# A two-layer Perceiver block on one core: the order of TensorE's work in the two cross attentions, and the contexts' layer norm on VectorE

## The chip, the core and the metric

The kernel runs on one core of one Trainium2 chip. Its time is the device time of one execution in microseconds (us). Before the change the median of three runs is 2801.76 us (2800.55 to 2803.31). The five engines are called PE (TensorE, matrix products and transposes), DVE (VectorE), ACT (ScalarE), POOL (GpSimd) and SP (SyncE, which here only starts DMAs).

## The reference

64 batches of 32 tokens of width 256 pass through six steps, each added to its input: a cross attention to 256 context rows (plus one row of its own kind, and the 32 tokens themselves), a self attention, a mixture of 64 experts, a second cross attention, a second self attention and a small feed-forward step. All of it is in 32-bit floats. What the change touches is this:

```
xn = layernorm(ctx, ln_x_g, ln_x_b)            # (x - mean) / sqrt(var + eps) * g + b, 256 wide
k, v from xn and from the layer-normed tokens   # 16 heads of 64
kn = k / max(norm(k) / 8, eps) * kn_g           # a norm for each key and head
attn = softmax(qn @ kn.T);  out = attn @ v
...
x = x + tanh(((x_normed @ weight) @ aux1) @ aux2 + bias)   # the last step; the three matrices are multiplied first
```

## The kernel before, in words

The 2048 tokens are 16 **tiles** of 128 (4 batches of 32 each). A batch with its context is a **sequence** `s`, 64 in all; `t, b = divmod(s, 4)`.

The order of PE's instructions is that of the program text (`manual_schedule` on PE). The order on the other engines and on SP's queue is made by a planner at compile time from a cost model: it puts an instruction earlier when its data and buffers are free in the plan. `nc.any` copies go to ACT or DVE as the planner finds them idle. Each engine then runs its own list strictly in order. All PSUM results share eight banks (`bank`), so a matmul also waits until the bank it gets has been emptied.

**First cross attention** (`before`, L381 to L510; `CrossFirst`). For each sequence: `load` (one 256 KB DMA), `prepare` (layer norm with scale and bias, in place, on DVE then POOL), `turn` (4 transposes, then copies to `xT`), `keys` (32 products into 8 banks, copied to `kT` by DVE and ACT alternately; ACT squares each half into `sq`; four small DMAs fill `c3`), `norms` (16 products over the squares, then `nk` on DVE and ACT), `spread` (8 products, ACT exponentials), `scores` (32 products, then softmax on DVE and ACT), `weigh` (12 transposes of the softmax, copied to `at`), `values` (8 products of 512 columns and 4 for the tail rows, copied to `yT`). The steps are staggered: iteration `s` weighs sequence `s` while it builds keys and scores of `s + 2`, turns `s + 3` and prepares `s + 4`.

Between these steps stand **slots**. A slot runs one step of each open generator: first the tails, then the fronts. A *tail* is what follows for a finished tile (output projection, self attention, routing); a *front* is the query side of the next tile. A tile has 11 slots in this loop. They are called A1 (between keys and norms), A2 (after spread) and A3 (at the end; not for `b = 3`). The steps of a tail of tile `t` that matter here, counted in slots from A1 of the next tile's `b = 0`: 1 output heads, 2 output product, 3 layer norm, 4 its transposes, 5 query, key and value products, 7 transposes of these (A1 of `b = 2`), 8 self-attention scores (L573, A2 of `b = 2`), 9 softmax scaling and 32x32 transpose (`eT`), 10 products with the values (L310, A1 of `b = 3`), 11 the projection, 12 to 14 routing.

For tile 14 of 16 a tail waits `HOLD` slots after its step 2, so that it runs nearer to tile 15's tail, which has no loop left beside it.

**Experts** (`experts`). 64 experts, with a shared expert's steps between. At `e == AHEAD` (12) `after_weights` loads and multiplies out the weights of what comes later: first the latent attention's (`latent_weights`), then the feed-forward matrices (`ffn_weights`, L1047), whose three DMA loads take the space the former just gave back.

**Second cross attention** (`after`, L806; `CrossSecond`). The same idea with fewer steps. An iteration runs: load, `scores(s + 2)` (16 products, four banks, each reduced by DVE and then exponentiated by ACT), slot S1, `weigh(s)` (12 transposes, `at` copied by ACT or DVE), slot S2, `values(s)` (8 products), slot S3. Its generators are `queries` (the query side, two tiles ahead) and `follow` (output projection, self attention and feed-forward of a finished tile, the latter's HOLD as above).

Of the kernel before, what the change touches and what calls it, by code (L numbers as in the profile page):

```python
# [10 lines left out]
F32 = mybir.dt.float32  # L11
# [3 lines left out]
ALU = mybir.AluOpType  # L15
AX = mybir.AxisListType

P = 128
D = 256
S = 32  # L20
# [3 lines left out]
H = 16  # L24
# [3 lines left out]
LAT = 32  # L28
# [1 line left out]
CAP = 128  # L30
GT = 4
AHEAD = 12
HOLD = 5
TOPK = 8
FI = 128
FS = 512
# [50 lines left out]
def done(steps):  # L87
    for _ in steps:
        pass


class Kernel:
# [116 lines left out]
            k0 += n  # L209
        return [at[:n, j, :] for j, n in enumerate(sizes)]  # L210

    def weighed(self, yT, b, at, values, tail=None):

        nc = self.nc
        ps = [self.bank("psY") for _ in range(2)]
        n = len(at)
        for kc in range(2):
            for i in range(n):  # L220
                nc.tensor.matmul(  # L221
                    ps[kc],
                    lhsT=values[i][:, kc * P : (kc + 1) * P],
                    rhs=at[i],
                    start=(i == 0),
                    stop=(i == n - 1 and tail is None),
                )
        if tail is not None:
            for kc in range(2):
                r = slice(64 * kc, 64 * kc + 64)  # L230
                nc.tensor.matmul(ps[kc], lhsT=tail[1][r, :], rhs=tail[0][r, :], start=False, stop=True)  # L231
        for kc in range(2):
            nc.any.tensor_copy(  # L233
                yT[:, kc, :, b * S : (b + 1) * S], ps[kc].rearrange("p (h i) -> p h i", h=H)
            )

    def heads_out(self, t, yT, wv, wo, bias, split=False):

# [52 lines left out]
    def attend_self(self, t, e, recip, wo, bias):  # L291

        nc = self.nc
        v = self.vz[t % 2]
        nc.vector.tensor_tensor(e, e, recip.unsqueeze(2).to_broadcast([P, H, S]), ALU.mult)  # L295
        eT = self.wk.tile([P, H, S], F32, name="eT", bufs=self.eb)
        nc.vector.transpose(eT.rearrange("p a b -> p (a b)"), e.rearrange("p a b -> p (a b)"))
        yield
        if self.slack:
            yield  # L300


        ps = [self.bank("psY") for _ in range(NB)]
        for k in range(2):
            for odd in range(2):
                for g in range(4):
                    h = 8 * k + 2 * g + odd
                    for b in range(NB):
                        r = slice(b * S, (b + 1) * S)
                        nc.tensor.matmul(  # L310
                            ps[b][g * 32 : (g + 1) * 32, k * S : (k + 1) * S],
                            lhsT=v[r, h, :, :].rearrange("p a b -> p (a b)"),
                            rhs=eT[r, h, :],
                            start=(odd == 0),
                            stop=(odd == 1),
                        )
        oT = self.wk.tile([P, 2, P], F32, name="oTs", bufs=self.vb)
        for b in range(NB):
            nc.any.tensor_copy(
                oT[:, :, b * S : (b + 1) * S], ps[b][:, : 2 * S].rearrange("p (k i) -> p k i", k=2)  # L320
            )
        yield
        ps = self.bank("psY")
        self.product(ps[:, :D], [oT[:, k, :] for k in range(2)], [wo[:, k, :] for k in range(2)])
        self.add_to_x(t, ps[:, :D], bias)
# [46 lines left out]
    def before(self, ctx):  # L372
# [3 lines left out]
        tc, nc, a = self.tc, self.nc, self.a  # L376
# [3 lines left out]
        w = self.pool(ctx, "w0", 1)  # L380
# [29 lines left out]
        ps = self.bank("psT")  # L410
# [9 lines left out]
        next(first)  # L420
        next(first)
        cross.prepare(1)
        for i in range(2):
            cross.load(i + 2)
            cross.turn(i)
            cross.keys(i)
            cross.norms(i)
            done(first)
            cross.spread(i)
            cross.scores(i)  # L430
        cross.load(4)
        cross.prepare(2)
        cross.prepare(3)
        cross.turn(2)

        wv = self.load(w, "wv", [P, 2, HD], a["a_wv"].rearrange("(k p) n -> p k n", p=P))
        wo = self.load(w, "wo", [P, 8, D], a["a_wo"].rearrange("(k p) n -> p k n", p=P))
# [38 lines left out]
        def slot():  # L476
            for q in (tails, fronts):
                for g in list(q):
                    if next(g, q) is q:
                        q.remove(g)  # L480

        for s in range(n):
            t, b = divmod(s, NB)
            next(zeros, None)
            if b == 0 and t + 3 < self.nt:
                self.tokens(t + 3)
            if b == 0 and t + 1 < self.nt:
                fronts.append(cross.queries(t + 1))
            if s + 5 < n:
                cross.load(s + 5)  # L490
            if s + 2 < n:
                cross.keys(s + 2)
            cross.weigh(s)
            slot()
            if s + 2 < n:
                cross.norms(s + 2)
            cross.values(s)
            if s + 2 < n:
                cross.spread(s + 2)
            slot()  # L500
            if s + 3 < n:
                cross.turn(s + 3)
            if s + 2 < n:
                cross.scores(s + 2)
            if s + 4 < n:
                cross.prepare(s + 4)
            if b == NB - 1:
                tails.append(self.tail(t, cross.yT, wv, wo, bo, sw, swo, sg, gw))
            else:
                slot()  # L510
# [5 lines left out]
    def tail(self, t, yT, wv, wo, bo, sw, swo, sg, gw):  # L516

        yield from self.heads_out(t, yT, wv, wo, bo, True)
        yield
        if t == self.nt - 2:  # L520

            for _ in range(HOLD):
                yield
        yield from self.self_first(t, sw, swo, sg)
        yield from self.route(t, gw)
# [130 lines left out]
    def experts(self, ctx, slot, tails):  # L656
# [94 lines left out]
        for e in range(E):  # L751
            weigh(e + AHEAD)
            fetch(e + 3)
            turn(e + 2)
            while (at - total + rest) * E < rest * e:
                next(side)
                at += 1
            inner(e + 1)
            outer(e)
            if e == AHEAD:  # L760
                self.after_weights()
        done(side)

        side, sums = shared(nt // GT - 1), self.combine(0)
# [32 lines left out]
    def after_weights(self):  # L797
        a, w = self.a, self.w2
        wq = self.load(w, "wq", [P, 2, HD], a["b_wq"].rearrange("(k p) n -> p k n", p=P))
        wkT = self.load(w, "wkT", [P, 8, D], a["b_wkT"].rearrange("(k p) n -> p k n", p=P))  # L800
        wv = self.load(w, "wv", [P, 2, HD], a["b_wv"].rearrange("(k p) n -> p k n", p=P))
        wo = self.load(w, "wo", [P, 8, D], a["b_wo"].rearrange("(k p) n -> p k n", p=P))
        bo = self.row(w, "bo", a["b_bo"], D)
        self.weights = wq, wkT, wv, wo, bo
        self.lat = self.latent_weights(w)
        self.ffnw = self.ffn_weights(w)  # L806

    def after(self, ctx):
        self.eb = self.vb = 1
# [15 lines left out]
        def slot():  # L825
            for g in list(steps):
                if next(g, steps) is steps:
                    steps.remove(g)
# [8 lines left out]
        for s in range(n):  # L837
            t, b = divmod(s, NB)
            if s + 3 < n:
                cross.load(s + 3)  # L840
            if s + 2 < n:
                cross.scores(s + 2)
            if b == NB - 2 and t + 2 < self.nt:
                steps.append(cross.queries(t + 2))
                if t + 3 < self.nt:
                    steps.append(self.combine(t + 3, 3))
            slot()
            cross.weigh(s)
            slot()
            if s < 2:  # L850

                slot()
                slot()
            cross.values(s)
            if b == NB - 1:
                steps.append(self.follow(t, cross.yT, wv, wo, bo))
            slot()
# [3 lines left out]
    def follow(self, t, yT, wv, wo, bo):  # L861

        yield from self.heads_out(t, yT, wv, wo, bo)
        if t == self.nt - 2:

            for _ in range(HOLD):
                yield
        yield from self.self_second(t, *self.lat)
        yield from self.ffn(t, *self.ffnw)
# [100 lines left out]
    def self_second(self, t, wl, bl, wvo, bvo, wqk, bqk, wo, bo):  # L970
        nc = self.nc
        _, zT = yield from self.normed(t)
        lat = self.wk.tile([P, 2 * H, LAT], F32, name="lat", bufs=1)
        latf = lat.rearrange("p h l -> p (h l)")
        for n in range(2):
            ps = self.bank("psA")
# [102 lines left out]
class CrossFirst:  # L1079
# [76 lines left out]
    def prepare(self, s):  # L1156

        k, nc, cx = self.k, self.k.nc, self.cx[s]
        k.layernorm(cx, cx)
        nc.gpsimd.tensor_tensor(cx, cx, self.gx.unsqueeze(1).to_broadcast([P, 2, D]), ALU.mult)  # L1160
        nc.gpsimd.tensor_tensor(cx, cx, self.bx.unsqueeze(1).to_broadcast([P, 2, D]), ALU.add)

    def turn(self, s):

# [110 lines left out]
        at = k.keyed(sim, [P, P, P])  # L1275
        self.weights = at[:2], [cx[:, 0, :], cx[:, 1, :]], (at[2], c3)

    def values(self, s):
        k = self.k
        b = s % NB  # L1280
        if b == 0:
            self.yT = k.wkx.tile([P, 2, H, P], F32, name="yT", bufs=1)
        k.weighed(self.yT, b, *self.weights)


class CrossSecond:
# [185 lines left out]
```

## Time and profile before

| what | value |
|---|---|
| profiled execution | 2804.67 us |
| its span (first to last instruction) | 2802.8 us, so 1.87 us lie around it |
| median of the runs | 2801.76 us |
| ACT, POOL busy | 1241.6 us (44%), 684.3 us (24%) |
| mean granted PE clock | 0.982 |
| first cross attention | about 0 to 1535 us |
| last tails, experts | about 1535 to 1800 us |
| second cross attention and the rest | about 1800 to 2803 us |
| PE busy, 160 to 1500 us | 1312.38 of 1340 us |
| PE busy, 1830 to 2700 us | 849.40 of 870 us |

A busy PE is not PE at its peak, since the ends of its matmuls are modelled: one matmul's modelled end lies past the start of the next. So where PE stalls, the idle time shown is a little less than the time lost, and the distance from one start to the next is the better measure. The granted clock says at what part of full speed PE was let run. Idle time of another engine costs nothing by itself; what it does to PE shows in the waits of PE.

### The profile page before, as it was taken

The numbers are of one execution on the slowest core, as the hardware profiler recorded it, in microseconds if no ns is written. First come the engines' busy times: TensorE is split into PE (matmuls) and PEld (weight loads), VectorE is DVE, ScalarE is ACT, GpSimd is POOL, SyncE is SP. The second block draws the span as 40 slices with busy tenths as digits, with TensorE's granted clock in tenths as the row PEclk, the third lists the DMA queues.
The fourth block names the chain that finished last, engine by engine and source line by source line (L and its number), as shares of the span: only waits on it lengthen the run. The fifth ranks groups of instructions, "written<-read, shape, count | busy, mean of one in ns | idle before, by whom it ended". The sixth has DMA issues, their size and how long they took to land. (4 is left out here: it accounts for less than half of the span.)

```text
span 2802.8 us, 58905 instructions
## 1 busy us (share of the span) xinstructions
PE 2657.6 (95%) x23386; PEld 1824.5 (65%) x23386; DVE 1694.9 (60%) x4427; ACT 1241.6 (44%) x3436; POOL 684.3 (24%) x756
## 2 busy tenths in 40 slices
PE   6999999999999999999999799999999999999996
PEld 3556666666666666666666578667777777777764
DVE  5546666666666666666665433466666666666664
ACT  3455555555555555555554223333333333333331
POOL 5211333133313331243121200321212222121001
PEclk8999999999999999999999899999999999999997
DMA  8000011011000000000001677321211222222110
GB/s 271 16 14 18 31 33 31 18 31 33 29 18 27 26 22 18 20 19 16 18 7 38 233 237 243 91 67 54 58 51 50 59 52 58 56 51 55 33 35 5
DMA packets 136087, 157.03 MB, mean 56 GB/s; under 512 B 24024, under 2 KB 118979, under 8 KB 135812
## 3 DMA queue, kind: packets, MB, share of 16 engines
q1 hardware_dynamic: 114308, 119.65, 13.8%
q0 software_dynamic: 12288, 25.21, 3.4%
q10 hardware_dynamic: 9216, 8.39, 0.9%
q8 instruction: 185, 3.03, 0.4%
q14 instruction: 90, 0.74, 0.1%
HBM read 121.63 MB, written 37.75 MB: 57 GB/s over the span
## 5 line engine op out<-in xcount | busy, mean ns | idle before, releaser
L167 PE MATMUL psA<-xT,wk 128*128 128x289 f32 x2048 | 517.4, 411 | 7.9 <-ACT xT L1176 4.5
L167 PEld LDWEIGHTS psA<-xT,wk 128*128 128x128 f32 x2048 | 388.0, 191 | 134.8 <-issue 21.8
L780 POOL DMA_INDIRECT y<-oute,idx x128 | 131.5, 1028 | 643.4 <-DVE x L791 453.9
L167 PE MATMUL psA<-at,cx 128*128 128x512 f32 x512 | 235.4, 602 | 20.0 <-ACT qTl L1005 18.2
L221 PE MATMUL psY<-at,cx 128*128 128x512 f32 x512 | 239.8, 612 | 0.1
L167 PE MATMUL psY<-xT,qk 128*128 128x257 f32 x1024 | 234.3, 382 | 0.0
L167 PEld LDWEIGHTS psY<-xT,qk 128*128 128x128 f32 x1024 | 190.8, 190 | 35.0 <-issue 10.2
L1357 DVE TENSOR_REDUCE mx<-psY 128x1 f32<-128x257 f32 x256 | 105.7, 423 | 133.6 <-PE psY L167 133.5
L1358 ACT ACTIVATE sim<-psY,mx 128x257 f32<-128x257 f32 x256 | 121.6, 476 | 142.3 <-DVE mx L1357 142.2
L184 ACT ACTIVATE sim<-sim,mx 128x289 f32<-128x289 f32 x256 | 134.1, 526 | 100.0 <-DVE mx L182 100.0
L221 PEld LDWEIGHTS psY<-at,cx 128*128 128x128 f32 x512 | 93.5, 192 | 123.0 <-issue 108.8
L167 PEld LDWEIGHTS psA<-at,cx 128*128 128x128 f32 x512 | 92.9, 190 | 120.8 <-issue 76.7
L233 ACT COPY yT<-psY 128x512 f32<-128x512 f32 x127 | 68.2, 589 | 220.7 <-PE psY L231 220.7
L645 POOL DMA_INDIRECT buf<-z,fi x128 | 126.5, 988 | 148.0 <-DVE fi L642 102.2
L1160 POOL TENSOR_TENSOR cx<-cx,a_gx 128x512 f32<-128x512 f32 x64 | 81.8, 1278 | 292.1 <-DVE cx L140 290.3
L1206 ACT ACTIVATE sq<-kT 128x1156 f32<-128x1156 f32 x128 | 149.4, 1167 | 4.4 <-DVE kT L1203 2.8
L1201 ACT COPY kT<-psA 128x289 f32<-128x289 f32 x256 | 94.8, 389 | 104.2 <-PE psA L167 104.2
L1376 ACT COPY at<-psT 128x512 f32<-128x512 f32 x145 | 78.8, 595 | 123.4 <-PE psT L1375 118.3
L1218 PE MATMUL psB<-sq,c 128*32 128x289 f32 x1024 | 109.4, 419 | 19.7 <-ACT sq L1206 19.5
L1388 DVE SCALAR_TENSOR_TENSOR yT<-at,xT,psA 128x512 f32<-128x512 f32 x128 | 94.0, 735 | 56.1 <-PE psA L167 50.7
L167 PE MATMUL psY<-yT,wv 128*64 128x128 f32 x2048 | 121.6, 275 | 1.6 <-DVE yT L1388 1.4
L1177 POOL COPY xT<-lnT 128x64 f32<-128x64 f32 x64 | 15.3, 240 | 423.0 <-PE psA L167 299.3
(257 smaller groups left out, 5190.5 us busy)
## 6 DMA issues: line engine op xcount, KB each, us to landing
cx<-in_ctx SPq DMA_DIRECT2D x128, 256.0 KB
we<-in_m_ew SPq DMA_DIRECT2D x64, 384.0 KB
xT<-in_ctxT SPq DMA_DIRECT2D x64, 257.0 KB
buf<-zero SPq DMA_DIRECT2D x32, 256.0 KB
be<-buf SPq DMA_DIRECT2D x64, 128.0 KB
oute<-oe ACTq DMA_DIRECT2D x64, 128.0 KB
mu<-in_mask SPq DMA_DIRECT2D x16, 128.5 KB
x<-in_x SPq DMA_DIRECT2D x16, 128.0 KB
```

Source lines behind the costliest of these rows:

```text
L167: self.nc.tensor.matmul(ps, lhsT=lhs[i], rhs=rhs[i], start=(i == 0), stop=(i == n - 1))
L184: nc.scalar.activation(sim[:, g, :], sim[:, g, :], AF.Exp, bias=mx[:, g : g + 1], accum_out=sm[:, g : g + 1])
L221: nc.tensor.matmul(ps[kc], lhsT=values[i][:, kc * P : (kc + 1) * P], rhs=at[i], start=(i == 0), stop=(i == n - 1 and tail is None),)
L645: d = nc.gpsimd.indirect_dma_start(out=self.buf[:, :], out_offset=bass.IndirectOffsetOnAxis(ap=fi[:, k : k + 1], axis=0), in_=z[:, 0, :], ...
L780: nc.gpsimd.indirect_dma_start(out=y, out_offset=None, in_=self.oute[:, :], in_offset=bass.IndirectOffsetOnAxis(ap=self.idx[:, t, k : k + ...
L1160: nc.gpsimd.tensor_tensor(cx, cx, self.gx.unsqueeze(1).to_broadcast([P, 2, D]), ALU.mult)
L1201: nc.scalar.copy(kT[:, p, :], ps[:, :JK])
L1206: nc.scalar.activation(sq[p // 4], kT[:, p - 3 : p + 1, :], AF.Square)
L1218: nc.tensor.matmul(ps[g * 32 : (g + 1) * 32, :JK], lhsT=k.pair[odd], rhs=sq[p // 4][:, p % 4, :], start=(odd == 0), stop=(odd == 1),)
L1357: nc.vector.tensor_reduce(mx[:, g : g + 1], ps[:, :J], AX.X, ALU.max, negate=True)
L1358: nc.scalar.activation(sim[:, g, :], ps[:, :J], AF.Exp, bias=mx[:, g : g + 1], accum_out=sm[:, g : g + 1])
L1388: nc.vector.scalar_tensor_tensor(self.yT[:, c, :, b * S : (b + 1) * S], self.at[:, 2, :].rearrange("p (h i) -> p h i", h=H), xT[:, c, J - ...
```

## The change

It has seven parts: the order of PE in the first cross attention's loop, with the values cut in two halves and the norms between them; the same work's start-up; the contexts' layer norm, whose scale and bias move from POOL into DVE's own operations; one more slot in the self attention of the first layer (`attend_self`); the two HOLD counts, with a second buffer for `lat`; the feed-forward weights, built at expert 24 instead of 12; and in the second cross attention, `weigh(s)` ahead of `scores(s + 2)`.

```diff
-HOLD = 5
+HOLD = 8, 9
...
-    def weighed(self, yT, b, at, values, tail=None):
+    def weighed(self, yT, b, kc, at, values, tail):
...
+        if kc == 0:
+            self.psy = [self.bank("psY") for _ in range(2)]
+        ps = self.psy
+        for i in range(len(at)):
+            nc.tensor.matmul(
+                ps[kc], lhsT=values[i][:, kc * P : (kc + 1) * P], rhs=at[i], start=(i == 0), stop=False
+            )
+        if kc == 1:
+            for c in range(2):
+                r = slice(64 * c, 64 * c + 64)
+                nc.tensor.matmul(ps[c], lhsT=tail[1][r, :], rhs=tail[0][r, :], start=False, stop=True)
...
@@ attend_self
         yield
-        if self.slack:
-            yield
+        yield
...
@@ before, start-up
-        for i in range(2):
-            cross.load(i + 2)
-            cross.turn(i)
-            cross.keys(i)
-            cross.norms(i)
-            done(first)
-            cross.spread(i)
-            cross.scores(i)
-        cross.load(4)
+        for i in range(2, 5):
+            cross.load(i)
+        cross.turn(0)
+        cross.keys(0)
+        done(first)
+        cross.turn(1)
+        cross.norms(0)
         cross.prepare(2)
+        cross.spread(0)
+        cross.scores(0)
+        cross.keys(1)
+        cross.turn(2)
+        cross.norms(1)
         cross.prepare(3)
-        cross.turn(2)
+        cross.spread(1)
+        cross.scores(1)
...
@@ before, the loop
+            cross.weigh(s)
             if s + 2 < n:
                 cross.keys(s + 2)
-            cross.weigh(s)
             slot()
+            cross.values(s, 0)
             if s + 2 < n:
                 cross.norms(s + 2)
-            cross.values(s)
+            cross.values(s, 1)
             if s + 2 < n:
                 cross.spread(s + 2)
...
@@ tail, follow
-            for _ in range(HOLD):
+            for _ in range(HOLD[0]):
...
-            for _ in range(HOLD):
+            for _ in range(HOLD[1]):
...
@@ experts, after_weights
+            if e == 2 * AHEAD:
+                self.ffnw = self.ffn_weights(self.w2)
...
-        self.ffnw = self.ffn_weights(w)
...
@@ after, the loop
-            if s + 2 < n:
-                cross.scores(s + 2)
...
             slot()
             cross.weigh(s)
+            if s + 2 < n:
+                cross.scores(s + 2)
             slot()
...
@@ self_second
-        lat = self.wk.tile([P, 2 * H, LAT], F32, name="lat", bufs=1)
+        lat = self.wk.tile([P, 2 * H, LAT], F32, name="lat")
...
@@ CrossFirst.prepare
-        k.layernorm(cx, cx)
-        nc.gpsimd.tensor_tensor(cx, cx, self.gx.unsqueeze(1).to_broadcast([P, 2, D]), ALU.mult)
-        nc.gpsimd.tensor_tensor(cx, cx, self.bx.unsqueeze(1).to_broadcast([P, 2, D]), ALU.add)
+        mv, rs = k.stats(cx, 2)
+        for j in range(2):
+            x = cx[:, j, :]
+            nc.vector.scalar_tensor_tensor(x, x, mv[:, j, 0:1], self.gx, ALU.subtract, ALU.mult)
+            nc.vector.scalar_tensor_tensor(x, x, rs[:, j : j + 1], self.bx, ALU.mult, ALU.add)
```

## The prediction

> **What bounds the kernel now.** I read the page's first two parts, then PE's waits, then the timeline around the longest of them.
>
> ```profile
> PE 2657.6 (95%) x23386; PEld 1824.5 (65%) x23386; DVE 1694.9 (60%) x4427; ACT 1241.6 (44%) x3436; POOL 684.3 (24%) x756
> PE   6999999999999999999999799999999999999996
> PEclk8999999999999999999999899999999999999997
> ```
>
> PE is the bound in every slice but the first, the last and the move to the experts. No edit removes a matmul, so a gain must come out of PE's idle time (2802.8 - 2657.6 = 145 us) or its half-clock time. The waits name the idle time (total, times, longest):
>
> ```profile
> PE psB L1218 <- ACT sq L1206: 19.5, 23, 2.1
> PE psA L167 <- ACT qTl L1005: 18.2, 12, 1.7
> PE psY L310 <- DVE at L208: 14.7, 14, 1.3
> PE psA L167 <- DMA f_a<-in_f_a: 4.8, 1, 4.8
> PE psB L573 <- ACT yT L233: 2.7, 14, 0.2
> ```
>
> Twelve to fourteen times means once a tile. The timeline (start, length, matmuls, idle before) shows the size, first cross attention first:
>
> ```profile
> 310.40 0.68 PE L1218 MATMUL psB<-sq,c 128*32 128x289 f32 x4
> 311.94 1.17 PE L1218 MATMUL psB<-sq,c 128*32 128x289 f32 x12 [0.86 <-ACT sq L1206]
> ...
> 330.72 0.26 PE L310 MATMUL psY<-eT,vz 32*32 32x32 f32 x6
> 332.01 1.24 PE L310 MATMUL psY<-eT,vz 32*32 32x32 f32 x122 [1.04 <-DVE at L208]
> 333.18 1.86 PE L1218 MATMUL psB<-sq,c 128*32 128x289 f32 x16
> ```
>
> The unbroken 16 take 1.86 us, the broken ones 2.71 (310.40 to 313.11): 0.85 lost. L310 takes 2.53 us here and 1.29 unbroken in the second layer: 1.24 lost. The second cross attention (weigh, values, then the next slot):
>
> ```profile
> 2252.83 1.48 PE L1375 MATMUL psT<-c,sim 128*128 128x128 f32 x12
> 2255.80 3.67 PE L167 MATMUL psA<-at,cx 128*128 128x512 f32 x8 [1.50 <-ACT qTl L1005]
> 2259.31 1.02 PE L167 MATMUL psB<-qTl,wqk 128*128 128x512 f32 x2
> 2260.17 0.60 PE L1014 MATMUL psT<-c,lat 128*128 128x128 f32 x4
> 2260.60 0.38 PE L149 MATMUL psT<-c,z 128*128 128x128 f32 x2
> 2260.82 3.64 PE L167 MATMUL psY<-xT,qk 128*128 128x257 f32 x16
> 2264.39 1.29 PE L1026 MATMUL psB<-kTl,qf 32*32 32x32 f32 x128
> ```
>
> Twelve transposes pace at 0.109, 1.31 in all; the values start 2.97 after them, so 1.66 is lost.
>
> **1. Loop order and the extra slot.** Before, keys, weigh, A1, norms; now weigh, keys, A1, first half of the values, norms. The norms' wait is for ACT's second square. At `b = 2` its cover after keys was weigh (1.31) and A1; now A1 and half the values (4 of 8 products at 0.43, 1.72). Scores also lie one weigh further from keys, so the softmax ahead of the square on ACT starts 1.31 earlier against keys. Together 1.7 us against 0.85: gone. What is late next is `b = 3`: A1 held L310, which moves to A2, so its cover is the half values alone. In the trace ACT ends that square at 333.82 (start 332.65, 1.17), with its exponentials back to back from 327.9. Keys would end near 330.9, the second norms start near 333.1: up to 0.7 comes back a tile. The split adds no change of PE's array shape: full to 32 columns and back happened once already. After the norms `nk` (DVE 0.46, ACT 0.45) has the second half (1.72) and the tail (1.13) as cover instead of 4.8; 2.9 suffices.
>
> L310's wait is for a bank that weigh's copies (L208) hold. In A2 it stands where L573 stands, behind spread with the values' copies just issued: that row costs 0.2. Its `eT` has a slot more. So 1.24 becomes about 0.25.
>
> Per tile: 1.0 + 0.85 - 0.35 (half of 0.7) = 1.5, times 14 = 21; I take **-20**, ends -28 and -5.
>
> **2. Layer norm on DVE.** Per context POOL loses 1278 + 1270 ns, which fed nothing late. DVE loses two tensor_scalars and gains four two-tensor operations; the nearest row is the experts' sum, same size, all in SBUF:
>
> ```profile
> L140 DVE TENSOR_SCALAR cx<-cx,mv,rs 128x256 f32<-128x256 f32 x128 | 61.8, 515 | 7.4 <-ACT rs L120 7.4
> L791 DVE SCALAR_TENSOR_TENSOR x<-y,w,x 128x256 f32<-128x256 f32 x128 | 59.8, 467 | 0.3
> ```
>
> 4 x 0.467 - 2 x 0.515 = 0.84 us, 54 us of DVE in all. The Trainium skill speaks against this: VectorE: DVE Perf Modes, The perf-mode tier table, has fp32 tensor_scalar in SBUF at two elements a cycle and the two-tensor operation at one. By it the removed pair would be worth about 2 x 0.23 and the addition 1.4 us, 90 in all. The row disagrees: median 411 ns with its pointer scalars, hardly under 467, and up to 1422 while POOL worked. I take the row. DVE is at 854 of 1340 us in this loop, so its cover is slack: **0**. Bounds: -13 (if the stretch of 515 over 411 is gone, 0.1 x 128, and had been on the path) and +54.
>
> **3. Start-up and first tile.** At 22.85 two tensor_scalars take 2.26 us beside POOL's multiply; the query sums on DVE, ACT's second query square and the copy to `xT` queue behind, and keys(0) starts at 26.97 after 3.40 idle, then partly at half clock (9.73 us for 32 products against 8.07). Without POOL I expect 2 of the 3.4 and 1.7 of clock back. keys(1) and keys(2) lose waits of 0.68 and 0.82 for `xT`, norms(0) its 1.08; spread(0) loses its cover (+1.1), norms(1) waits more for a softmax now closer. The loads of contexts 2 to 4 go ahead of keys' eight `c3` DMAs and the mask on SP, 768 KB at 271 GB/s, 2.8 us, wanted late. **-6**, ends -11 and +2.
>
> Until tile 0's tail exists no slot has filler: from 70 to 160 us PE idles 9.4, on squares (0.80, 1.98, 0.80, 2.10) and on `xT` before keys (0.75, 0.65, 1.80, 0.54), and the clock falls twice:
>
> ```profile
> 119.84:123.25 3.41, 1.53 (x16) 0.54 (x16) 1.56 (x3) 2.98 (x5) 1.39 (x2) 1.00 0.12 39
> 123.25:126.66 3.41, 3.41 (x8) 1.42 (x5) 0.46 (x1) 0.45 (x1) 0.36 (x3) 0.50 0.00 0
> ```
>
> (PE busy is the third number, clock third from the end.) The Trainium skill (TensorE: Matmul & The Clock Gate, Part 1) halves the clock after an idle window of about 3.4 us; by that, stalls of 2 us would cost only themselves, 9.4. Here a window with PE busy 1.53 of 3.41 was enough, and eight values take 5.16 instead of 3.70: 1.5 more, twice. Half the values now cover the squares and weigh covers `xT`: 12.4 at most; **-7**, ends -11 and -3.
>
> **4. Feed-forward weights.** The 4.80 idle, then half clock (16 products in 6.25 us against 3.6), sum 7.4. The three loads issue at 1628.5, when the latent weights free their space; SP's planner had brought the latent loads forward by some 60 us (1552), so at expert 24, over 30 us later, these have landed. A copy of `mid` (0.37) shows now, 0.5. **-7**; 0 if they stay at their place in the text behind the expert loads.
>
> **5. weigh before scores.** Scores (3.64) stand between weigh and values, and ACT's `at` copies no longer queue behind the exponentials: 12 x 1.66 + two short ones, -21. But S3 and S1 now touch. At `b = 2` to `3`, `kTl` (0.16 for the last transpose to end, 0.1 to signal, copy 0.59) has only L149's two transposes (0.22) before L1026: 0.6; at `b = 0` to `1`, `zT` waits likewise before the latent products. The nearest row, at the end of the kernel, has transposes at 2756.72 and products at 2757.62 0.90 from start to start less 0.22 of their own; less another tile's two transposes, 0.5. So 1.1 x 13 = 14 comes back: **-7**, ends -21 and +3.
>
> **6. HOLD and lat.** Tile 14's steps move nearer tile 15's, but ahead of them in each slot: its query or latent products (2.75 and 4.6 us) now delay tile 15's output product by what the loop saves. Beside the softmax (idle 6.15 and 7.53) more of tile 14 stands, on a DVE both share. The second `lat` only makes this overlap possible. **0** and **+1**, each -4 to +5.
>
> Sum: -20 + 0 - 6 - 7 - 7 - 7 + 0 + 1 = -46. The profiled 2804.67 becomes 2759; the median of the runs lies 2.9 lower: **2756**.
>
> **Rivals.** *Nothing comes back*: part 5 whole (-21): 2742. For: ACT is idle at S3; against: the copies have latency. *Half is given back*: part 1 brings 10 only, since `b = 3` pays its 0.7 and other norms wait too (+10); start-up brings 1 (+5), the two ends cost 6 more: 2777. For: softmax and squares share ACT; start-up is full of DMA (271 GB/s). *Slower*: DVE queues are planned, and the four operations (1.9 us) can stand before the key copies or `nk`. At 327.83 DVE copies keys PE began at 321.4, so there it is late. In half the 64 contexts that is 61 us: 2817; it decides from 24 contexts (46 / 1.9). Against: only `b = 2` and `3` are that tight. *The loads are not brought forward*, so that part 4 does nothing: 2763, inside the first case.
>
> **Chances.** About 2756 (2744 to 2769) 0.45; nothing back 0.13; half back 0.27; slower 0.12; within 0.2% (about what a measurement can tell) 0.03. Faster 0.85. The range 2730 to 2792 leaves out the slower cases.
>
> **What would show it.** Right: L310's wait under 4 us in all, no `f_a` wait, `qTl` gone from PE's waits, `kTl` and `zT` in its place near 14 us; L1218 under 10; DVE near 1750 busy, POOL near 520. Wrong: PE waiting for key copies or `nk`; a new wait on `at` or banks at weigh; a half clock at 55 us as before.

## The result, and the profile after

The changed kernel takes 2813.70 us (median of six, 2811.40 to 2815.39) against 2801.61 for the kernel before (six runs): 1.0041 times as long, 95% interval 1.0028 to 1.0053. It was forecast 46 us faster and is 12 slower. First its page: span, busy time and the PE rows of the 40 slices.

```profile
span 2812.1 us, 59021 instructions
...
PE 2655.0 (94%) x23386; PEld 1823.0 (65%) x23386; DVE 1664.0 (59%) x4432; ACT 1306.7 (46%) x3559; POOL 552.9 (20%) x628
...
PE   6999999999999999999997899899999999999995
...
PEclk9999999999999999999998899999999999999996
```

The matmuls are the same 23386. PE's idle time (span less busy) has grown from 145.2 to 157.1 us. Of the clock's dips at the start only the one near 55 us is left, half as long (the clock from 50 to 70 us was 0.66 and is 0.83); those at the move to the experts and at the end have stayed. PE's waits (total, times, longest):

```profile
PE psT L149 <- DVE z L140: 28.1, 9, 6.4
PE psB L1223 <- ACT sq L1211: 24.2, 33, 2.3
PE psB L1029 <- DVE qf L1014: 18.2, 13, 3.8
...
PE psY L306 <- issue: 4.3, 4, 1.8
PE psA L167 <- issue: 4.1, 3, 1.7
PE psB L575 <- issue: 3.9, 1, 3.9
...
PE psY L306 <- ACT yT L230: 3.4, 14, 0.2
...
PE psT L207 <- DVE qk L541: 3.2, 11, 0.5
```

L310 is now L306, and its 14.7 us on `at` are 3.4. `qTl` and `f_a` are gone. But the norms (L1218, now L1223) wait 24.2 instead of 19.5, `qf` takes exactly the 18.2 that `qTl` had, and "issue" appears: PE waits for nothing that the profile shows. Before, that was 3.4 us in all.

Where the time went, by the start of the same PE work in both traces (after less before, us):

| marker | difference | so this stretch |
|---|---|---|
| output heads of tile 0 (at 166 before) | -16.0 | start-up and tile 0: -16.0 |
| output heads of tile 14 (1475) | -12.7 | 14 tiles of the first loop: **+3.3** |
| output heads of tile 15 (1526) | -15.7 | here HOLD puts off steps of tile 14: -3.1 |
| first shared expert (1568) | -5.8 | last tails: **+9.9** |
| first scores of the second loop (1786) | -9.9 | experts: -4.0 |
| values of sequence 60 (2717) | -0.6 | second loop: **+9.2** |
| end of PE (2794) | +9.2 | last tails: **+9.9** |

So the start gave what was forecast (13) and 3 more, the experts a little over half of their 7; the first loop, put at -20, gave nothing, and three places lost. Its quiet tiles are 0.1 us shorter than before on average, but four others (tiles 2, 3, 8 and 13) 0.6 to 1.4 longer. Here is a tile of the first loop, from keys to scores at `b = 3` (timeline of PE after):

```profile
499.61 4.31 PE L167 MATMUL psA<-xT,wk 128*128 128x289 f32 x17
503.76 1.88 PE L222 MATMUL psY<-at,cx 128*128 128x512 f32 x4
505.57 0.68 PE L1223 MATMUL psB<-sq,c 128*32 128x289 f32 x4
507.04 1.17 PE L1223 MATMUL psB<-sq,c 128*32 128x289 f32 x12 [0.79 <-ACT sq L1211]
...
511.81 0.28 PE L306 MATMUL psY<-eT,vz 32*32 32x32 f32 x6
512.34 1.40 PE L306 MATMUL psY<-eT,vz 32*32 32x32 f32 x122 [0.25 <-ACT yT L230]
```

Between the last key product and the norms there is only the half of the values: A1 is empty. The norms take 2.64 us from 505.57 to their end. Unbroken they take 1.19, which the prediction had not seen: its "unbroken" 1.86 already held 0.67 of a wait that the modelled ends hide.

The losses of a quiet tile (from the output heads of tile 5 to those of tile 6; norms: start to end less 1.19; L306: start to the next instruction less 1.22), in us, are these. `old_dve` (the kernel before with the layer norm on DVE) and `order_again` (the changed kernel without the slot, with the old HOLD and the old second loop) are told of below:

| | before | `old_dve` | after | `order_again` |
|---|---|---|---|---|
| norms at b = 2 | 1.36 | 1.01 | 0.28 | 0 |
| norms at b = 3 | 0.67 | 0.67 | **1.45** | 0.03 |
| norms at b = 0 | 0 | 0 | 0 | 0 |
| norms at b = 1 | 0.65 | 0.66 | **1.10** | 0 |
| L310 / L306 | 1.24 | 1.24 | 0.65 | 0 |
| weigh, for a bank | 0 | 0 | 0.41 | 0 |
| sum | 3.92 | 3.58 | 3.89 | 0.03 |
| the whole tile | 93.54 | 93.19 | 93.40 | 89.97 |

Differences of the sums follow those of the tiles within 0.4 us. The changed kernel moved 3.9 us of stalls about and removed almost none.

### The profile page after: what moved, and what is told of

Same layout as the page of the kernel before. It is cut to its first block, busy times and chain, and to the rows that moved or that the text cites. A ratio compares the mean times of both kernels' runs of the same rounds, so it can differ in the third digit from the quotient of the medians.

```text
span 2812.1 us, 59021 instructions
## 1 busy us (share of the span) xinstructions
PE 2655.0 (94%) x23386; PEld 1823.0 (65%) x23386; DVE 1664.0 (59%) x4432; ACT 1306.7 (46%) x3559; POOL 552.9 (20%) x628
## 5 line engine op out<-in xcount | busy, mean ns | idle before, releaser
L167 PE MATMUL psA<-xT,wk 128*128 128x289 f32 x2048 | 510.8, 407 | 1.3 <-issue 1.1
L222 PE MATMUL psY<-at,cx 128*128 128x512 f32 x512 | 248.6, 609 | 0.0
L1223 PE MATMUL psB<-sq,c 128*32 128x289 f32 x1024 | 99.8, 415 | 24.2 <-ACT sq L1211 24.2
L167 PEld LDWEIGHTS psY<-yT,wv 128*64 128x64 f32 x2048 | 113.2, 137 | 9.7 <-issue 4.8
L167 PE MATMUL psY<-wo,oT 128*128 128x256 f32 x512 | 118.8, 386 | 0.3 <-issue 0.3
L1272 DVE TENSOR_TENSOR sim<-psB,sim 128x289 f32<-128x289 f32 x256 | 101.2, 448 | 29.2 <-PE psB L1263 29.1
```

The source lines that it names most:

```text
L167: self.nc.tensor.matmul(ps, lhsT=lhs[i], rhs=rhs[i], start=(i == 0), stop=(i == n - 1))
L222: nc.tensor.matmul(ps[kc], lhsT=values[i][:, kc * P : (kc + 1) * P], rhs=at[i], start=(i == 0), stop=False)
L1223: nc.tensor.matmul(ps[g * 32 : (g + 1) * 32, :JK], lhsT=k.pair[odd], rhs=sq[p // 4][:, p % 4, :], start=(odd == 0), stop=(odd == 1),)
L1272: nc.vector.tensor_tensor(sim[:, g, :], ps[i][:, :JK], sim[:, g, :], ALU.mult)
```

## The experiments

Each run is compared with the kernel before on the same chip; "ratio" is that comparison with its 95% interval, and a hundredth of it is 28 us.

**HOLD alone undone** (`hold5`).

```diff
-HOLD = 8, 9
+HOLD = 5, 5
```

> The changed kernel with both HOLD counts at 5 again, all else as changed. Theory H (the longer HOLDs put tile 14's steps in front of tile 15's): the move to the experts gives back 8 to 10 us and the end another 8 to 10, so 2795 (2790 to 2801). Rival (the two ends lose by PE's code fetch, wherever the dense bursts fall): some 'issue' waits move, the time stays within 5 us of 2814.

2797.3 us, ratio 0.9977 [0.9967, 0.9986]: 18 less than the changed kernel (1.0041). Its last stretch loses 0.3 us against the kernel before, where the changed kernel loses 9.9. Step 6, put at 0 and +1, costs 18.

**The second loop's order undone** (`second_old`).

```diff
+            if s + 2 < n:
+                cross.scores(s + 2)
             if b == NB - 2 and t + 2 < self.nt:
...
             cross.weigh(s)
-            if s + 2 < n:
-                cross.scores(s + 2)
```

> The changed kernel with scores(s + 2) ahead of the first slot again in the second cross attention, all else as changed. Theory as predicted blind (weigh first is worth 7): 2821, PE waits 1.5 us a tile for at behind qTl. Theory now (weigh first gains 0.2 us a tile and then loses 10 to code fetch and the half clock behind it): 2804 (2800 to 2810), with no wait on qf at L1029 and tiles of 61.5 us without outliers.

2805.5 us, ratio 1.0006 [0.9997, 1.0015]: the new order costs 10 where it was to gain 7. All tiles take 61.53 to 61.55 us. With the new order (timeline of PE after), where the third column is the engine and the bracket the idle time before:

```profile
2125.68 1.02 PE L167 MATMUL psB<-qTl,wqk 128*128 128x512 f32 x2
2126.53 0.60 PE L1017 MATMUL psT<-c,lat 128*128 128x128 f32 x4
2126.97 0.38 PE L149 MATMUL psT<-c,z 128*128 128x128 f32 x2
2128.56 1.28 PE L1029 MATMUL psB<-kTl,qf 32*32 32x32 f32 x128 [1.20 <-DVE qf L1014]
2129.76 0.82 PE L167 MATMUL psA<-zT,wq 128*128 128x128 f32 x5
2132.31 4.79 PE L167 MATMUL psA<-zT,wq 128*128 128x128 f32 x27 [1.73 <-issue]
```

S3 and S1 touch, as foreseen, and the latent scores (L1029) wait; but it is `qf` that comes last, which DVE makes from the product at 2125.68, and not `kTl` or `zT`. So a quiet tile takes 61.37 us, 0.17 less than before. The 1.73 <-issue behind them is the other loss: six of the tiles take 62.4 to 65.0. Each of the six has one such wait, 7.3 us in all, and behind two of them (at 2132 and 2279 us) the clock is 0.50 for 3.4 us.

**A slot between latent keys and latent scores** (`second_slack`), HOLD 5 and 5, to give that wait its cover.

```diff
         nc.any.tensor_copy(kT, ps)
         yield
+        yield
```

> The changed kernel with HOLD 5 and 5, and one more slot between the copies of the latent keys and the latent scores; the second loop keeps its new order (weigh ahead of scores). Theory (qf's wait, 1.20 us in 13 tiles, came back only because slots S3 and S1 now touch): the wait goes, quiet tiles fall from 61.4 to 60.2, 2797 - 15 = 2782, with some tiles still 1 to 3 us longer for PE's own instructions. Rival (another wait takes its place, z, zT or the copies' bank): quiet tiles stay at 61.4 and the time at 2797.

2797.4 us, ratio 0.9981 [0.9974, 0.9988]: the rival. `qf` is gone from PE's waits, but two others stand in its place, and all tiles but one take 61.97:

```profile
PE psA L167 <- ACT zT L150: 17.5, 31, 0.7
...
PE psY L167 <- DVE yT L1393: 7.4, 15, 0.9
```

It looks as if, with S3 and S1 together, some step of the tail always stands too near to its data; that is argued from these waits alone.

**32 tiny products in front** (`pad32`), all else equal, to see what "issue" is. The trace shows them as 64 products and 64 weight loads.

```diff
-        ps = self.bank("psT")
+        ps, i = self.bank("psT"), self.ident[:32, :32]; [nc.tensor.matmul(ps[:32, 256:288], lhsT=i, rhs=i, start=True, stop=True) for _ in range(32)]
```

> The changed kernel with 32 tiny products (128 PE instructions[...]) put in front of the first transpose, where PE idles for 16 us anyway; the order on every engine is otherwise the same. Theory F (the 'issue' waits of PE are waits for its code): the waits leave tiles 2, 3, 8 and 13 of the first loop and turn up in other tiles, and the sum over the kernel changes; total 2805 to 2822. Rival (they are waits for data that the profile does not name): the same tiles are long by the same 1.4 us, total 2814 within 2.

2807.7 us, ratio 1.0015 [1.0006, 1.0023]. The long tiles of the first loop were tiles 2, 3, 8 and 13; now they are 5 and 10. In `hold5`, `second_old`, `second_slack` and `best`, which leave PE's order in this loop as it is, tiles 2, 3, 8 and 13 are long again, with one or two others. In the second loop some moved too, and the longest "issue" wait of L306 is now 3.5 us. Nothing that depends on data was changed: where the stalls fall hangs on where an instruction lies in PE's program. The page of the changed kernel has the row for it (packets, MB, share):

```profile
q8 instruction: 185, 3.03, 0.4%
```

2 x 23386 products and weight loads in 185 packets would be 253 each, if these packets carry PE's instructions. L306 and L1029 are each 128 products and 128 weight loads in 1.3 us: by this estimate a whole packet. That PE then waits for the next one is an inference from this count and from the shift; no run measured a fetch by itself. And such a burst alone is not enough: `order_again`, below, has the same bursts, and "issue" stands at 1.9 us in all there, against 20.3 in the changed kernel.

**The layer norm back on POOL** (`pool_norm`), in the changed kernel.

```diff
-        mv, rs = k.stats(cx, 2)
-        for j in range(2):
...
+        k.layernorm(cx, cx)
+        nc.gpsimd.tensor_tensor(cx, cx, self.gx.unsqueeze(1).to_broadcast([P, 2, D]), ALU.mult)
+        nc.gpsimd.tensor_tensor(cx, cx, self.bx.unsqueeze(1).to_broadcast([P, 2, D]), ALU.add)
```

> The changed kernel with the contexts' scale and bias back on POOL, all else as changed. Theory D (the four operations on DVE, and ACT's rs behind them, hold up the second square at b = 1): the wait of 0.44 us before the norms of b = 1 goes, 8 us in all, and the start-up loses 3 to 5: 2810. Rival (the norm on DVE costs the loop nothing, as predicted): the loop keeps its 93.4 us a tile and only the start-up loses: 2818.

2849.3 us, ratio 1.0159 [1.0139, 1.0179]: 33 slower than the changed kernel, and no theory had that. A new wait stands first among PE's:

```profile
PE psR L1242 <- ACT nk L1230: 38.0, 15, 2.8
```

At one of these, DVE's timeline (start, length) shows two products of the layer norm taking 2.57 us together, and two small operations of the routing 0.97 and 1.05, all while POOL multiplies and adds (371.55 to 377.1):

```profile
371.75 2.57 DVE L140 TENSOR_SCALAR cx<-cx,mv,rs 128x256 f32<-128x256 f32 x2
...
374.84 0.97 DVE L631 TENSOR_TENSOR val<-val,kept 128x64 f32<-128x64 f32 x1
...
376.11 1.05 DVE L636 SCALAR_TENSOR_TENSOR junk<-val,v,pr 128x64 f32<-128x64 f32 x1
...
377.24 0.27 DVE L636 SCALAR_TENSOR_TENSOR junk<-val,v,pr 128x64 f32<-128x64 f32 x1
...
379.07 0.46 DVE L1229 TENSOR_SCALAR nk<-psB 128x289 f32<-128x289 f32 x1
```

The same L636 takes 0.27 once POOL is done. `nk`, whose products ended at 374.3, comes 4.8 us late. By these lines the stretch makes up some 3.3 of that (1.75 of L140, as two of them take 0.82 alone, 0.76 of L631 and 0.78 of L636); the rest is the routing that stands ahead of `nk` in DVE's list. In the changed kernel PE's waits for `nk` are 2.1 us in all. Only this one place was taken apart.

**The layer norm on DVE alone, in the kernel before** (`old_dve`: in `prepare` alone, as in the diff of the change).

> The kernel before with part 2 alone: scale and bias of the contexts' layer norm in four DVE operations instead of two on DVE and two on POOL. Moving them back to POOL in the changed kernel cost 35 us. Theory (in the old order the norms stand 1.3 us later behind the softmax and nk has a cover of 4.8 us, so DVE's stretch beside POOL costs nothing there): 2803 within 4, tiles 93.5. Rival 1 (the stretch costs in the old order too): 2790 or less. Rival 2 (the four operations stand ahead of key copies): 2812 or more.

2790.3 us, ratio 0.9956 [0.9940, 0.9973]: 12 faster, rival 1. 7.7 of it are there by sequence 8; then tiles of 93.19 instead of 93.54 give the rest. Of the norms' wait at `b = 2` 0.35 goes, since the softmax ahead of ACT's second square is through 0.35 sooner.

**Both losing parts undone** (`best`: HOLD 5 and 5, second loop old).

> Both parts that cost time are undone: HOLD is 5 in both places and in the second cross attention the scores stand ahead of slot S1 again. The kernel before ran at 2803.5. Theory (the two losses are separate and add up: HOLD 16, measured 2797.3 when undone alone; the order of the second loop 8 to 10): 2797 - 9 = 2788, second-loop tiles all near 61.5 us. Rival (they overlap, or the second loop's qTl wait only returns what HOLD gave): 2796 or more.

2787.1 us, ratio 0.9945 [0.9928, 0.9961]: the two losses add up.

**The first loop in its old order on top of that** (`best_old1`): keys, weigh, A1, norms, whole values, L306 in A1.

> As the run with both parts undone, and also the first cross attention's loop in the old order (keys, weigh, A1, norms, whole values) without the extra slot in the first layer: part 1 of the prediction is taken out, the start-up, the layer norm on DVE and the later feed-forward weights stay. Theory A (part 1 brings nothing in a quiet tile, 93.4 against 93.5 us, and costs about 5 us of tiles in which PE waits for its own instructions): 2783, 5 faster than with the new order, L1218's norms wait near 19 us and L310's wait near 14 us in PE's waits again. Theory B (part 1 does pay some 10 us, masked by the layer norm's four DVE operations): 2798. Prediction on record: 20 slower than with the new order, 2808.

2784.2 us, ratio 0.9938 [0.9922, 0.9955]: theory A. Taken whole, part 1 brings nothing that can be told from the noise.

**The new order in tile 0 alone** (`hybrid`).

```diff
+            if s < NB:
+                cross.weigh(s)
             if s + 2 < n:
                 cross.keys(s + 2)
+            if s >= NB:
+                cross.weigh(s)
...
```

> The new order of the first loop in its first four iterations only (tile 0, where no tail fills the slots), the old order and the old slot after that; HOLD 5 and the old second loop as before. Theory (part 3's gain is 12 with the new order in tile 0 and 8 without it, and the rest of part 1 brings nothing): 2784.2 - 4 = 2780, tiles after the first 93.19. Rival (the gain of tile 0 is only a shift that the next tile gives back): 2784.

2780.6 us, ratio 0.9924 [0.9908, 0.9941]: in tile 0, without tails, the order does earn its 4. The intervals alone would not tell this from `best_old1`; the traces do, which differ by 5.4 us at the keys of sequence 8 and by 4.1 at the end.

**Copies to `at` on DVE** (`best_at`).

```diff
-            nc.any.tensor_copy(at[:n, j, :], ps[:n, :])
+            nc.vector.tensor_copy(at[:n, j, :], ps[:n, :])
```

> The run with both parts undone (2787.1), and weigh's three copies to at fixed on DVE, where in the new order the planner has put most of them on ACT (ACT is busy 782 us between 160 and 1500 us, against 735 in the old order). Theory G (these copies keep ACT from the squares, which is why the norms wait 24.3 us in the new order and 15.0 in the old): the norms' wait falls below 15, tiles from 93.4 to 92.9 or less, 2787 - 8 = 2779. Rival (the cover after keys is what is too short, whoever copies; and the copies now stand in DVE's list behind its mask, maximum and key copies): the norms' wait stays above 20 or moves to key copies and at, 2787 to 2800.

2778.9 us, ratio 0.9921 [0.9902, 0.9940]: the time is the theory's, but the norms still wait 22.1, 21 times instead of 33. The stall at `b = 1` (0.44) went; that at `b = 3`, seen above, grew from 0.79 to 1.00. Between two engines that both feed the squares the load only moves.

**The extra slot in the old order** (`slot_only`: L306 from A1 to A2).

> The first loop in the old order, but with the first layer's extra slot, so that only L306 (the self attention's products with the values) moves from A1 to A2. Without the slot this kernel ran at 2784.2, with tiles of 93.19 us and L306 waiting 14.4 us on at. Theory (the two halves of part 1 pull apart: the extra slot pays its 1.0 a tile, the order takes it back in norms): L306's wait below 4, tiles 92.2, 2784 - 14 = 2770, less what PE waits for its own instructions. Rival (where L306 leaves A1, the norms behind it lose their cover in the old order as well): the norms' wait rises from 15 to 25 or more, tiles 93.2 or longer, 2784 or slower.

2853.8 us, ratio 1.0188 [1.0170, 1.0205]: 70 slower than without the slot, beyond even the rival. In PE's waits, L1223 stands at 70.4 us, 63 times: at every `b` but 0, and twice at `b = 3`. There PE goes from weigh straight to the norms (timeline):

```profile
425.29 1.47 PE L207 MATMUL psT<-c,sim 128*128 128x128 f32 x12
427.21 0.68 PE L1223 MATMUL psB<-sq,c 128*32 128x289 f32 x4 [0.45 <-ACT sq L1211]
...
429.84 0.45 PE L1223 MATMUL psB<-sq,c 128*32 128x289 f32 x4 [1.95 <-ACT sq L1211]
```

At `b = 3` the norms begin 9.83 us after keys instead of 11.76, while ACT's second square ends 12.41 after them in both kernels: L306 in A1 was the norms' cover. At the other two `b` the square itself ends 0.8 to 1.2 us later. L306's own wait did fall, from 14.4 to 3.4.

**The slot alone taken out** of the new order: with both losing parts undone (`order_only`), the same with `at` on DVE (`order_at`), and in the changed kernel itself (`after_noslot`).

```diff
         yield
-        yield
+        if self.slack:
+            yield
```

> The run with both parts undone (2787.1), without the extra slot of the first layer: the loop keeps its new order (weigh, keys, A1, half values, norms), but L306 is back in A1 of b = 3. Theory S (weigh now stands a whole keys ahead of A1, so L306's wait for the bank goes by the order alone; the slot only took 2.5 us of cover from the norms at b = 3): L306's wait stays below 4, the norms' loss at b = 3 (1.46 us from first to last product beyond the 1.19 of unbroken ones) goes, 1.2 to 1.5 a tile, 2787 - 20 = 2767. Rival (the tail's later steps each stand one slot earlier and open a hole elsewhere, or L306 waits in A1 again): 2784 or slower.

> As the run before it, and weigh's copies fixed on DVE (with the slot that brought 8: 2778.9). Theory S: both add up, since the copies cost at other places of the tile as well: 2778.9 - 18 = 2760. Rival (the copies on DVE had helped just where the slot hurt): the same as without the slot and with the planner's choice, 2767.

> The changed kernel itself with the extra slot alone taken out; HOLD 8 and 9 and the new second loop stay. The changed kernel ran at 2813.7. Theory S: 20 less, 2794, which with the 16 of HOLD and the 10 of the second loop would be the whole way to about 2767. Rival: 2813.

2766.5, 2774.1 and 2785.8 us, ratios 0.9793 [0.9776, 0.9809], 0.9815 [0.9799, 0.9832] and 0.9860 [0.9844, 0.9877]. On this chip the kernel before took 2825.8. By these ratios the slot costs 43 in `order_only` (0.9945 to 0.9793) and 51 in the changed kernel (1.0041 to 0.9860), where theory S said 20. `at` on DVE now costs 8, so neither case of `order_at` held. Without the slot the changed kernel would have been faster than before.

**Once more, and HOLD 8 at the first end** (`order_again`, `hold85`), on another chip.

> The changed kernel without the extra slot, HOLD 5 and 5, the second loop in its old order, run beside the kernel before once more: in the earlier run (2766.5) the kernel before took 2825.8 us, though it takes 2802 to 2804 everywhere else. If that was a trait of the chip that both kernels shared, the ratio stays at 0.979; if only the kernel before was slower there, 2766.5 / 2802 = 0.987.

> The same kernel with HOLD 8 for the first loop's end, 5 for the second's. Theory (the first loop's end lost 10 us only because the extra slot added to the tail: without the slot, from the start of tile 15's output heads to the shared expert the kernel with HOLD 8 lost 6.1 us against the kernel before and that with HOLD 5 8.2, and tile 15's heads began 3.1 earlier): 2766.5 - 5 = 2761. Rival (HOLD 8 costs there whatever the slot, and what the experts' start gains is given back by its DMAs): 2766 to 2776.

2732.4 us, ratio 0.9750 [0.9737, 0.9763], and 2738.0, ratio 0.9769 [0.9756, 0.9783]. HOLD 8 at the first end costs 5.6 by itself: the rival. `order_again` beats both kernels by far; its tiles take 89.97 us, to 0.01. Its page and the PE timeline at `b = 3`:

```profile
span 2731.8 us, 58984 instructions
...
PE 2622.0 (96%) x23386; PEld 1806.2 (66%) x23386; DVE 1651.4 (60%) x4446; ACT 1306.5 (48%) x3545; POOL 532.0 (19%) x628
```

```profile
393.01 7.97 PE L167 MATMUL psA<-xT,wk 128*128 128x289 f32 x32
400.92 1.29 PE L306 MATMUL psY<-eT,vz 32*32 32x32 f32 x128
402.13 1.98 PE L222 MATMUL psY<-at,cx 128*128 128x512 f32 x4
404.05 1.23 PE L1223 MATMUL psB<-sq,c 128*32 128x289 f32 x16
405.21 1.98 PE L222 MATMUL psY<-at,cx 128*128 128x512 f32 x4
```

No wait in brackets is left. L306 needs no wait in A1, because the copies to `at` were begun a whole keys (8 us) earlier, and with the half values it gives the second square 3.1 us.

## Why the prediction was wrong, step by step

Three runs between the two kernels share out the whole (us, measured by the ratios; a step of less than about 6 can't be told from the noise):

| from, to | what is added | forecast | measured |
|---|---|---|---|
| before, `best_old1` | layer norm (2), start-up (3), feed-forward weights (4) | -13 | -17 |
| `best_old1`, `best` | first loop's order and slot (1), and so tile 0 (3) | -27 | +2 |
| `best`, `hold5` | second loop's order (5) | -7 | +9 |
| `hold5`, after | HOLD and `lat` (6) | +1 | +18 |

**Step 1 (-20) failed, and cost most.** Its sentence "L310's wait is for a bank that weigh's copies (L208) hold. In A2 it stands where L573 stands" gave the credit to the slot. The slot does end this wait (`slot_only`), but the order does it alone (`order_again`), since weigh moves ahead of keys: the slot was not needed. What it costs is in the prediction's own words: at `b = 3` "its cover is the half values alone". There "up to 0.7 comes back" was 0.78 (0.67 to 1.45), the right place and size; half of it was booked. Missed were four things: another 0.45 at `b = 1`, where the planner's lists end the second square 11.3 us after the start of keys, against 9.6 without the slot; 0.41 for a bank at weigh; L306 at 0.65 where a loss of 0.25 was put; and what the order could have had at `b = 3` and `b = 1`, since 1.86 was read as unbroken. Order and slot apart: the order alone earns 53 (0.9938 to 0.9750), the slot costs 55 (0.9750 to 0.9945); on the chip of `order_only` these are 41 and 43 (0.9938 to 0.9793 to 0.9945).

**Step 2 (0) was wrong to the good side.** The norm on DVE earns 12 in the old order; under the changed order, taking it away costs 33. The bound of -13 was for the stretch of L140 beside POOL if it "had been on the path", and its size came out. But of the 12, 4.6 come in tile 0 from sequence 4 to 6, where the prediction had put the norm at nothing, and at `b = 2` the stretched operation is not L140 but L118, a small one of the query side that stands ahead of the softmax in DVE's list: 0.81 us beside POOL's multiply (at 579.64 before), 0.18 in `old_dve` (at 570.75). By the rule of the Trainium skill (VectorE: DVE Perf Modes, The perf-mode tier table) the exchange was estimated to add 90 us of DVE work, by the prediction's row 54. It added 83: the new operations take 145.2 us in all, L140 took 61.8. That this is near the page's estimate is chance: their medians, 478 and 480 ns, are near the row's 467, and the means of 611 and 549 hold single ones stretched to as much as 2.09 us; and L140's median of 411 was not half of that. DVE's busy time still fell, from 1694.9 to 1664.0 where 1750 was forecast, because the planner moved 91 us of copies to `at` from DVE to ACT (whose busy time rose from 1241.6 to 1306.7). The rival *slower* came near in time (2817 against 2813.7), not in cause.

**Step 3 (-6 and -7) was right in size**: in `hybrid`, -13.5 at the keys of sequence 8. `old_dve` has 7.7 of it from the norm, `best_old1` 0.4 more from the new start-up, and `hybrid` 5.4 more from the order. PE was busy 80.58 of the 90 us from 70 to 160 before, and the clock was 0.96; after (PE busy second, clock third from the end):

```profile
70.00:160.00 90.00, 85.98 (x575) 50.80 (x578) 44.37 (x103) 50.45 (x128) 11.12 (x15) 1.00 0.07 19
```

By the states that the Trainium skill tabulates (TensorE: Matmul & The Clock Gate, Part 1: half speed after an idle window of about 3.4 us) there was no clock to gain, as no stall there was longer than 2.1 us; the trace shows 0.04 of 90, 3.6 us. But `old_dve`, in the old order, has a clock of 1.00 there too: that part of step 3 belongs to the norm. The half clock "at 55 us as before", a sign of being wrong, was half as long as before.

**Step 4 (-7) was right.** From the first shared expert to the second loop's first scores, `best_old1` gains 6.6 on the kernel before and `old_dve`, with the weights at their old place, loses 1.0. The changed kernel gains only 4.0 there, `hold5` 7.5: the difference goes with HOLD.

**Step 5 (-7) had its sign wrong.** The term "1.1 x 13 = 14 comes back" measured 18.2, and on `qf` (1.20 a time and 3.8 at the end), which the prediction did not name; as much came back as went with `qTl`. The missing term is the six long tiles, 12 us above the quiet ones in all, with an "issue" wait in each, whose cause is open.

**Step 6 (0 and +1) measured 18.** By the markers of `hold5` against the changed kernel, 7 of it are there at the second loop's first values and 10 come in the last tails. The gain that was hoped for did come: more of tile 14 stands beside the softmax, and PE's waits for it (`eT`) fall by 10.5. What failed is the balance: tile 15's product was to be delayed "by what the loop saves", which put the net cost at nothing. In `hold5` two of PE's waits were

```profile
PE psT L149 <- DVE z L140: 20.2, 8, 6.4
...
PE psY L306 <- DVE eT L294: 13.7, 3, 7.5
```

and in the changed kernel `eT` has 3.2, but `z` 28.1, `qf` 3.6 and "issue" 8.7 more than there. The clock falls with it. At the end of the kernel, before and after (PE busy second, clock third from the end):

```profile
2700.00:2812.00 112.00, 75.42 (x992) 51.94 (x990) 51.07 (x108) 21.12 (x62) 9.65 (x9) 0.84 0.03 10
```

```profile
2700.00:2812.00 112.00, 78.44 (x993) 54.18 (x991) 49.36 (x106) 21.11 (x61) 9.64 (x9) 0.78 0.03 10
```

PE is busy 3 us longer for the same work. In the last tails of the first loop, PE after:

```profile
1533.10 1.12 PE L554 MATMUL psT<-c,qk 128*128 128x128 f32 x4 [3.56 <-POOL qk L542]
...
1540.29 0.48 PE L575 MATMUL psB<-kbd,qT 32*32 32x64 f32 x19 [3.92 <-issue]
1545.75 0.66 PE L149 MATMUL psT<-c,z 128*128 128x128 f32 x2 [2.97 <-DVE z L140]
```

Two tails close together may wait for the same engines in step, and L306 stands next to L575. That the stalls come from the nearness is argued; that HOLD costs the 18 is shown.

Rivals: *half is given back* named the right place for part 1 but ended at 2777. What the profile was to show as right did show for L306, `f_a`, `qTl` and, nearly, POOL (552.9 for 520); L1223 at 24.2 instead of under 10, DVE at 1664 and a new wait for a bank at weigh (3.2) were the signs against.

## What to carry over

When a wait goes because its releaser was moved earlier, don't also move the waiter later: it may have been somebody's cover. Count for each slot what stands in it after the move, by sequence, against the time that the engine behind the next wait needs. And take the unbroken length of a burst from its shortest instance anywhere in the trace, not from one without a bracket.

## What the hardware showed

- Operations of DVE between SBUF and SBUF took up to four times as long beside POOL's element-wise work (1.05 us instead of 0.27 for L636, 0.81 instead of 0.18 for L118, 2.57 instead of 0.82 for two of L140), so POOL's work had a price on DVE.
- PE stalled up to 3.9 us without a visible releaser at or behind bursts of short products, at places that 128 instructions more in front moved about. With the same bursts `order_again` has 1.9 us of this in all; the cause is open.
- In the last tails the granted clock fell with the stalls: from 2700 us on it was 0.84 before and 0.78 after, and the same products kept PE busy 3 us longer.
- On one chip the kernel without the slot was 34 us slower (2766.5) than on another (2732.4), with the same instructions in the same order and the first tiles alike. From the heads of tile 2 on its tiles take 92.2 us instead of 90.0, and `nk` waits 27.9 us there in all instead of 2.1. Its DVE at `b = 1`, then the other chip's:

```profile
362.05 0.88 DVE L1166 SCALAR_TENSOR_TENSOR cx<-cx,rs,a_bx 128x256 f32<-128x256 f32 x2
367.26 0.46 DVE L1231 TENSOR_SCALAR nk<-psB 128x289 f32<-128x289 f32 x1 [4.33 <-PE psY L228]
```

```profile
362.58 0.88 DVE L1166 SCALAR_TENSOR_TENSOR cx<-cx,rs,a_bx 128x256 f32<-128x256 f32 x2
363.70 0.46 DVE L1231 TENSOR_SCALAR nk<-psB 128x289 f32<-128x289 f32 x1 [0.24 <-PE psB L1223]
```

`nk` began only some 1.3 us after the last of eight indirect DMAs of POOL, which took as long on both chips. Why on that chip alone stays open; the kernel before was slower there too, by 24 us, so the ratios of its three runs are nearer the truth than their times.
